# Where independent matmuls stand between an attention's score passes: a set length behind the second scores, and one whole product in every step of the second batch

## The chip, the cores and the metric

One core of one Trainium2 chip runs the program. The metric is device time of one execution in microseconds (us), median of three runs. The profile is one further execution, taken by the hardware profiler. Engines: TensorE (PE; PEld is its weight load), VectorE (DVE), ScalarE (ACT), GpSimd (POOL), SyncE (SP, which only issues DMAs here). PSUM has eight banks of 128 x 512 float32; matmuls write there, VectorE and ScalarE read from there.

## The reference

Input x is 2 batches x 1024 tokens x 1024 channels, all float32.

```python
xn = layernorm(x)                                   # no weights
q, k, v = split(clip(xn @ Wqkv.T, -8, 8))           # each 1024 channels
q, k = layernorm(q) * q_w + q_b, layernorm(k) * k_w + k_b
scores = q_h @ k_h.T * 32**-0.5 + slope_h * (kpos - qpos)   # 32 heads of 32, causal
attn = (softmax(scores) @ v_h) @ Wout.T
ffn = xn @ (mean|W| * sign(W)).T + bias             # W = weight_real, 1024 x 1024
out = x + attn + ffn
```

## The kernel before

Everything is written for one order, laid out by hand: the program issues its instructions in the order in which they shall stand on each engine, and tiles in rotating buffers add the waits.

**The attention** works in blocks (b, qb, g): batch, half of the queries (512) and group of four heads. Four heads of 32 channels stand in the four row strips of TensorE, so that their matmuls run side by side. A block passes twice over its scores. `first_scores` (matmuls at L1006) takes scores of 128 queries against up to 512 keys, four PSUM banks for the four heads, and VectorE finds the row maxima from them (L1025, a custom add-and-max reduction). `shifts` (L1037) turns the maxima into rows of shifts, with small GpSimd operations and a transpose (L1052). `second_scores` makes the scores again, with keys on the partitions (L1067), adds the shifts by tiny matmuls (L1081), masks the diagonal on VectorE (L1100), and ScalarE takes the exponentials into tiles `pT` (L1109, 16 buffers). GpSimd adds those up for the denominators (L1138; VectorE in the very last block). `weigh_values` multiplies `pT` by the values (L1149). `divide` sums over partitions with a matmul `den` (L1168), and ScalarE and GpSimd divide.

**The step loop** (from L1228) takes these units in turn. In step n stand, in this order: the first scores of unit n; `divide` if a block has ended; `weigh_values` of unit n - LAG - 1; the second scores of unit n - LAG, with LAG = 9; and calls of `fill`. Two attention units of different blocks are paired into one where each has less than a bank.

**The fillers.** Everything else on TensorE is a stream of pieces, the generator `pieces`: the projections k, q, v of both batches, then the binarized linear layer, then the output projection. The projections use a seven-product scheme (`seven`, L396): a pair of token tiles needs seven products instead of eight, each of four matmuls of 128 x 128 by 128 x 512 (L402) into one PSUM bank, and VectorE combines them (L433, L444). The linear layer (`mm_f`, L793) has 16 matmuls for one product, in four pieces. `held` is true while a product is half done. `fill(time)` (L903) draws pieces until their estimated costs have used up the time, and every second piece advances the side chains (layer norms, transposes, loads). With `whole` it goes on until the product in hand is done. Overdrawn time is carried over, so a call of `fill` can draw nothing at all.

How much is filled: in the first batch's steps (n < middle = 81), `free` is what an equal share leaves beside the step's own attention work. `BEFORE` = 0.4 of it goes between first and second scores, the rest behind the second scores. In later steps a fixed time `each` goes behind the second scores, nothing between. At the end `fill(inf)` draws all that is left; the last two pairs of the output projection (14 products) need the last block, so they stand there anyway.

**PSUM.** Seven banks (`ps_s`) are shared by first scores (four at a time), second scores (four), the product in hand, transposes and denominators; one bank holds the attention's output. A bank comes free when VectorE or ScalarE has read it.

**Other queues.** SP issues loads in the program's order: q, k and v groups (L930, L934, L943), weights into a ring (L213), and attention outputs back from DRAM for the output projection (L844).

Of the kernel before, what the change touches and what calls it, by code (L numbers as in the profile page):

```python
# [25 lines left out]
def parallel_block_kernel(  # L26
# [49 lines left out]


    ONE, SHORT, TURN = 0.915, 1.03, 0.55
    BEFORE = 0.4
    PART, FOLD, SWITCH = 0.95 / 512, 0.3 / 512, 0.1  # L80
    QK_SCALE = HEAD_DIM ** (-0.5)
    slopes = [2.0 ** (-(h + 1) * ALIBI_BIAS_MAX / N_HEADS) for h in range(N_HEADS)]
# [253 lines left out]
    def advance_sides():  # L336
        time = 0.0
        for s in list(sides):
            cost = next(s, None)
            if cost is None:  # L340
                sides.remove(s)
            else:
                time += cost
        return time
# [49 lines left out]
    held = [False]  # L394
# [498 lines left out]
    def pieces():  # L893
        for b in range(B):
            yield from keys_or_queries("k", b)
            yield from keys_or_queries("q", b)
            yield from values(b)
        yield from binary_linear()
        yield from output()

    left = {"pieces": pieces(), "time": 0.0, "owed": 0.0}

    def fill(time, whole=False, sides_too=True):  # L903

        left["time"] += time
        while left["time"] > 0.0 or (whole and held[0]):
            cost = next(left["pieces"], None)
            if cost is None:  # L910
                left["time"] = 0.0
                break
            left["owed"] += 0.5
            left["time"] -= cost
            if sides_too and left["owed"] >= 1.0:
                left["owed"] -= 1.0
                left["time"] -= advance_sides()

    def fill_until(what):
        while what not in done:  # L920
            left["time"] = 0.0
            fill(0.01)
# [5 lines left out]
    def load_keys(b, qb, g):  # L928
        q = group.tile([P, HALF], FP, tag="q", name=f"qg_{b}_{qb}_{g}", bufs=6)
        nc.sync.dma_start(q, qd[b][g][:, half(qb)])  # L930
        k = []
        for n in range(qb + 1):
            k.append(group.tile([P, HALF], FP, tag="k", name=f"kg_{b}_{qb}_{g}_{n}", bufs=6))
            nc.sync.dma_start(k[n], kd[b][g][:, half(n)])  # L934
        st["q", b, qb, g], st["k", b, qb, g] = q, k

    def load_values(b, qb, g):
        v = []
        for n in range(qb + 1):
            v.append(  # L940
                group.tile([P, NQ, P], FP, tag="v", name=f"vg_{b}_{qb}_{g}_{n}", bufs=4)
            )
            nc.sync.dma_start(  # L943
                v[n],
                vd[b][half(n), g * P : (g + 1) * P].rearrange("(t p) d -> p t d", p=P),
            )
        st["v", b, qb, g] = v

    def open_block(*block):
        st[("mx",) + block] = small.tile(  # L950
            [P, G, NQ], FP, tag="mx", name="mx_{}_{}_{}".format(*block), bufs=3
        )
# [44 lines left out]
    def first_scores(unit):  # L997

        name = "s1_{}_{}_{}_{}_{}".format(*unit[0][0], *unit[0][1:3])
        banks = [score_bank(f"{name}_{j}") for j in range(G)]  # L1000
        c0 = 0
        for block, i, k0, n in unit:
            q, k = st[("q",) + block], st[("k",) + block][k0 // HALF]
            for j in range(G):
                r = slice(32 * j, 32 * j + 32)
                nc.tensor.matmul(  # L1006
                    banks[j][:, c0 : c0 + n],
                    q[r, tokens(i - block[1] * NQ)],
                    k[r, :n],
                    start=True,  # L1010
                    stop=True,
                )
            c0 += n
        for j in range(G):
            c0 = 0
            for block, i, k0, n in unit:
                at = i - block[1] * NQ
                o0 = S - (i + 1) * P + k0
                m = st[("mx",) + block][:, j, at : at + 1]
                sums = work.tile(  # L1020
                    [P, HALF], FP, tag="sums", name=f"sums{name}_{j}_{c0}", bufs=1
                )
                opened = ("max", block, j, i) in st
                st["max", block, j, i] = True
                nc.vector.tensor_tensor_reduce(  # L1025
                    out=sums[:, :n],
                    in0=banks[j][:, c0 : c0 + n],
                    in1=rel[:, o0 : o0 + n],
                    scale=1.0,
                    scalar=m if opened else LOWEST,  # L1030
                    op0=ALU.add,
                    op1=ALU.max,
                    accum_out=m,
                )
                c0 += n

    def shifts(b, qb, g):  # L1037

        mx = st.pop(("mx", b, qb, g))
        sh = small.tile([P, G, NQ], FP, tag="sh", name=f"sh_{b}_{qb}_{g}", bufs=2)  # L1040
        nc.gpsimd.tensor_tensor(sh, mx, pos, ALU.add)
        nc.gpsimd.tensor_scalar(sh, sh, -1.0, None, ALU.mult)
        sb = shift_b.rearrange("p i (j r) -> p j i r", j=G)
        for n in range(3):
            nc.gpsimd.tensor_copy(sb[:, :, :, n], sh)
            if n < 2:
                nc.gpsimd.tensor_tensor(sh, sh, sb[:, :, :, n], ALU.subtract)
        yield True

        ps = ps_s.tile([P, NQ, P], BF, tag="s", name=f"trs_{b}_{qb}_{g}")  # L1050
        for i in range(NQ):
            nc.tensor.transpose(ps[:, i, :], shift_b[:, i, :], ident_b)  # L1052
        rows = small.tile([P, HALF], BF, tag="rows", name=f"rows_{b}_{qb}_{g}", bufs=4)
        nc.scalar.copy(rows, ps.rearrange("p i q -> p (i q)"))
        st["rows", b, qb, g] = rows
# [107 lines left out]
    def divide(b, qb, g):  # L1163

        ps = score_bank(f"den_{b}_{g}_{qb}")
        total = st.pop(("sum", b, qb, g))
        for j in range(G):
            nc.tensor.matmul(  # L1168
                ps[32 * j : 32 * j + 32, :],
                ones,  # L1170
                total[j],
                start=True,
                stop=True,
            )
        inv = work.tile([P, HALF], FP, tag="inv", name=f"inv_{b}_{g}_{qb}", bufs=1)
        nc.scalar.activation(inv, ps, AF.Ln)
        nc.scalar.activation(inv, inv, AF.Exp, scale=-1.0)  # L1177
        ot = st["ot", b, qb, g]
        if (b, qb, g) == blocks[-1]:
            nc.vector.tensor_tensor(ot, ot, inv, ALU.mult)  # L1180
        else:
            nc.gpsimd.tensor_tensor(ot, ot, inv, ALU.mult)  # L1182
            nc.gpsimd.dma_start(od[b][g][:, half(qb)], ot)
        done.add(("o", b, qb, g))
# [32 lines left out]
    def short_lead(block):  # L1217

        return block[1] == 1 and block[2] == 0
# [3 lines left out]
    for n in range(3):  # L1223
        if n in opens:
            load_keys(*opens[n])
    fill(proj - AHEAD * ONE)
    chains = []
    for n in range(steps + 1):  # L1228
        if n + 3 in opens and not short_lead(opens[n + 3]):
            fill_until(("q", opens[n + 3][0]))  # L1230
            load_keys(*opens[n + 3])
        if n + 2 in weighs:
            block = weighs[n + 2]
            fill_until(("v", block[0]))
            load_values(*block)
        if n in opens:
            open_block(*opens[n])
        if n < len(first):
            first_scores(first[n])
        closing = shifts(*closes[n]) if n in closes else None  # L1240
        if closing:
            next(closing)
        m = n - LAG
        if m - 2 in ends:
            divide(*ends[m - 2])
        free = max(share - time_of(n), 0.0)
        if n < middle:
            fill(free * BEFORE, sides_too=False)
        if 0 <= m - 1 < len(second):
            weigh_values(second[m - 1], ends.get(m - 1))  # L1250
        if 0 <= m < len(second):
            second_scores(second[m])
        for c in chains:
            next(c, None)
        chains = [closing] if closing else []
        if n + 2 in opens and short_lead(opens[n + 2]):
            fill_until(("q", opens[n + 2][0]))
            load_keys(*opens[n + 2])
        if n < middle:
            fill(free * (1.0 - BEFORE))  # L1260
        else:
            fill(each, whole=True)
    fill(float("inf"))
# [51 lines left out]
```

## Time and profile before

| | |
|---|---|
| median of 3 runs | 1578.15 us (1576.8 to 1581.82) |
| the profiled execution's own time | 1580.05 us |
| its span, first to last instruction | 1578.3 us |
| mean granted TensorE clock | 0.992 |
| busy: PE, DVE, ACT, POOL | 1553.1, 909.5, 688.5, 998.8 us |

The span begins with the first projection (to about 350 us, with the first first scores from 278 us on), goes on with the first batch's attention over the projections of the second batch (to about 955 us), then the second batch's attention over the linear layer (to about 1235 us) and over the output projection (to about 1520 us), and ends with the last 14 or 15 products. A group of matmuls in the timeline is drawn from its first start to its last end, waits inside it included.

### The profile page before, as it was taken

What the parts mean: (1) busy time and instruction counts of PE and PEld (TensorE: products, weight loads), DVE (VectorE), ACT (ScalarE), POOL (GpSimd) and SP (SyncE); (2) the same over time, 40 slices, a digit from 0 to 9 for tenths busy, and PEclk for the clock granted to TensorE, in tenths of its full rate; (3) what the DMA queues carried; (4) which work ended last, traced back from release to release, by engine and by line L of the source; (5) the groups of instructions that cost most, each with busy time, mean ns of one, the idle gap of its engine ahead of it and who ended that gap; (6) DMA issues with size and microseconds to landing.
All of it is one profiled execution on the core that took longest, in us unless ns stands there. A gap on an engine that the chain in (4) does not pass through costs nothing.

```text
span 1578.3 us, 25307 instructions
## 1 busy us (share of the span) xinstructions
PE 1553.1 (98%) x8452; PEld 682.3 (43%) x8452; DVE 909.5 (58%) x2602; ACT 688.5 (44%) x1425; POOL 998.8 (63%) x1306
## 2 busy tenths in 40 slices
PE   7999999999999999999999999999999999999998
PEld 3444444444444434333333344555555433333343
DVE  7745353766676666666666555656555556555232
ACT  2553341114665645545542374545444434434420
POOL 4473071024675566676566599887798988778841
PEclk9999999999999999999999999999899999999999
DMA  7776364592323655558742377656565831233232
GB/s 290 295 254 261 100 206 151 185 324 74 107 95 112 224 191 182 131 129 253 249 159 94 115 250 221 140 130 136 134 147 97 225 87 39 77 81 74 57 78 53
DMA packets 116466, 244.94 MB, mean 155 GB/s; under 512 B 10544, under 2 KB 50992, under 8 KB 113008
## 3 DMA queue, kind: packets, MB, share of 16 engines
q1 hardware_dynamic: 88752, 145.01, 27.8%
q0 software_dynamic: 27584, 98.32, 24.0%
q8 instruction: 67, 1.10, 0.3%
q14 instruction: 63, 0.52, 0.1%
HBM read 155.47 MB, written 107.74 MB: 167 GB/s over the span
## 4 chain that ended last, share of the span: by engine, by line
PE 65%; DVE 1%; POOL 1%; issue 1%; ACT 1%; DMA 0%; POOLq 0%; DVEq 0%; ACTq 0%
PE s L1006 9%; PE s L1067 9%; PE o L1149 8%; PE mm_f L793 8%; PE mm_o_t L402 7%; PE mm_o L402 5%; PE mm_q_t L402 4%; PE mm_v_t L402 4%; PE mm_q L402 3%; PE mm_v L402 3%; PE den L1168 2%; PE s L1081 2%; PE mm_k_t L402 1%; PE mm_k L402 0%; PE tr_q L506 0%
## 5 line engine op out<-in xcount | busy, mean ns | idle before, releaser
L1138 POOL TENSOR_TENSOR pT<-pT,pT 128x512 f32<-128x512 f32 (+3 forms) x628 | 579.9, 983 | 101.8 <-ACT pT L1109 100.9
L1109 ACT ACTIVATE pT<-s,kpos 128x512 f32<-128x512 f32 (+3 forms) x768 | 378.2, 590 | 464.5 <-DVE s L1100 274.1
L1025 DVE CUSTOM_DVE_ANT_0 sumss<-s,rel 128x512 f32<-128x512 f32 (+2 forms) x284 | 179.1, 631 | 112.4 <-PE s L1006 79.3
L1006 PE MATMUL s<-kg,qg 32*128 32x512 f32 (+3 forms) x1536 | 197.3, 523 | 0.7 <-ACT kT L570 0.6
L1067 PE MATMUL s<-qg,kg 32*128 32x512 f32 (+3 forms) x1536 | 176.7, 525 | 1.3 <-DVE mx L1025 1.3
L1149 PE MATMUL o<-pT,vg 128*32 128x512 f32 (+3 forms) x1536 | 155.3, 499 | 0.0
L793 PE MATMUL mm_f<-sg,hl 128*128 128x512 f32 x512 | 128.6, 403 | 2.1 <-DVE mx L1025 2.1
L1006 PEld LDWEIGHTS s<-kg,qg 32*128 32x128 f32 x1536 | 80.0, 183 | 110.4 <-issue 44.8
L1100 DVE TENSOR_TENSOR s<-s,behind 128x256 f32<-128x256 f32 (+1 forms) x320 | 96.9, 371 | 48.1 <-PE s L1081 47.9
L402 PE MATMUL mm_o_t<-w_o_t,ot 128*128 128x512 f32 x256 | 116.6, 602 | 0.0
L1067 PEld LDWEIGHTS s<-qg,kg 32*128 32x128 f32 x1536 | 71.7, 185 | 101.4 <-issue 56.3
L1182 POOL TENSOR_TENSOR ot<-ot,inv 128x512 f32<-128x512 f32 x31 | 39.5, 1273 | 114.3 <-ACT inv L1177 114.3
L402 PE MATMUL mm_k_t<-w_k_t,xT 128*128 128x512 f32 x224 | 110.7, 614 | 0.5 <-DVE mx L1025 0.4
L793 PEld LDWEIGHTS mm_f<-sg,hl 128*128 128x128 f32 x512 | 94.7, 190 | 34.4 <-DVE mx L1025 10.6
L402 PE MATMUL mm_q_t<-w_q_t,xp 128*128 128x512 f32 x224 | 108.2, 605 | 0.0
L402 PE MATMUL mm_v_t<-w_v_t,xp 128*128 128x512 f32 x224 | 106.3, 606 | 0.1
L402 PE MATMUL mm_k<-w_k,xT 128*128 128x512 f32 x192 | 91.4, 616 | 0.9 <-DVE mx L1025 0.7
L402 PE MATMUL mm_v<-w_v,xp 128*128 128x512 f32 x192 | 89.6, 604 | 0.0
L1149 PEld LDWEIGHTS o<-pT,vg 128*32 128x32 f32 x1536 | 37.3, 109 | 119.1 <-issue 102.8
L402 PE MATMUL mm_q<-w_q,xp 128*128 128x512 f32 x192 | 88.7, 603 | 0.0
L402 PE MATMUL mm_o<-w_o,ot 128*128 128x512 f32 x192 | 87.5, 602 | 0.1
L1025 DVE CUSTOM_DVE_ANT_0 umss<-s,rel 128x512 f32<-128x512 f32 x100 | 69.2, 692 | 26.1 <-PE s L1006 15.3
(222 smaller groups left out, 2009.0 us busy)
## 6 DMA issues: line engine op xcount, KB each, us to landing
xp<-xd SPq DMA_DIRECT2D x16, 1792.0 KB, 8.3
kg<-kd SPq DMA_DIRECT2D x48, 256.0 KB, 5.0
vg<-vd SPq DMA_DIRECT2D x48, 256.0 KB, 7.9
wd_ot<-in_wout_t_dram POOLq DMA_DIRECT2D x11, 1024.0 KB, 9.4
xd<-xT POOLq DMA_DIRECT2D x8, 1280.0 KB, 5.3
x<-in_x_dram SPq DMA_DIRECT2D x16, 512.0 KB, 6.3
kd<-kT POOLq DMA_DIRECT2D x16, 512.0 KB, 4.1
qd<-qT POOLq DMA_DIRECT2D x16, 512.0 KB, 4.2
```

The costliest lines, as they stand in the source:

```text
L402: nc.tensor.matmul(ps, pr[:, FACTOR[block], c, :], W[what, block, c], start=(c == 0), stop=(c == NI - 1),)
L793: nc.tensor.matmul(ps, hl[c // NI][:, m % 2, c % NI, :].bitcast(FR), sg[n, c], start=(m == 0), stop=(m == 2 * NC - 1),)
L1006: nc.tensor.matmul(banks[j][:, c0 : c0 + n], q[r, tokens(i - block[1] * NQ)], k[r, :n], start=True, stop=True,)
L1025: nc.vector.tensor_tensor_reduce(out=sums[:, :n], in0=banks[j][:, c0 : c0 + n], in1=rel[:, o0 : o0 + n], scale=1.0, scalar=m if opened els ...
L1067: nc.tensor.matmul(banks[j][:, c0:c1], k[r, tokens(kt % NQ)], q[r, q0:], start=(c0 == 0), stop=False,)
L1081: nc.tensor.matmul(banks[j][:, c0:c1], ones_b[r, :], rows[r, q0:], start=False, stop=(c1 == HALF or (block, kt, q0) == unit[-1]),)
L1100: nc.vector.tensor_tensor(at, at, mask, ALU.add)
L1109: nc.scalar.activation(pT[:, c0:c1], banks[j][:, c0:c1], AF.Exp, bias=kpos[:, h, a : a + 1], scale=slopes[h],)
L1138: eng.tensor_tensor(part_sum, part_sum, pT[j], ALU.add)
L1149: nc.tensor.matmul(po[32 * j : 32 * j + 32, q0:], v[:, kt % NQ, 32 * j : 32 * j + 32], pT[j], start=(kt == 0), stop=(last is not None and ...
L1168: nc.tensor.matmul(ps[32 * j : 32 * j + 32, :], ones, total[j], start=True, stop=True,)
L1182: nc.gpsimd.tensor_tensor(ot, ot, inv, ALU.mult)
```

## The change

Three edits, all in how the stream of pieces is dealt out. In the first batch, the fill behind the second scores gets a set length `LATER` = 4.0 (in the estimate's us, or all of `free` where that is less), and the rest goes between first and second scores. In the second batch, a call with `whole` draws at least one piece, and so at least one whole product, whatever time was overdrawn before. No instruction is added or removed; they stand in another order.

```diff
-    BEFORE = 0.4
+    LATER = 4.0
...
         left["time"] += time
-        while left["time"] > 0.0 or (whole and held[0]):
+        none = whole
+        while left["time"] > 0.0 or none or (whole and held[0]):
+            none = False
             cost = next(left["pieces"], None)
...
         free = max(share - time_of(n), 0.0)
         if n < middle:
-            fill(free * BEFORE, sides_too=False)
+            fill(max(free - LATER, 0.0), sides_too=False)
...
         if n < middle:
-            fill(free * (1.0 - BEFORE))
+            fill(min(free, LATER))
         else:
             fill(each, whole=True)
```

## The prediction

> **What bounds the kernel now.** I read the page first, then the granted clock by stretches, then TensorE's timeline step by step, and last the end of the run. TensorE counts as busy nearly all the time:
>
> ```profile
> PE 1553.1 (98%) x8452; PEld 682.3 (43%) x8452; DVE 909.5 (58%) x2602; ACT 688.5 (44%) x1425; POOL 998.8 (63%) x1306
> ```
>
> All of its work is the same before and after, so only its stalls can change. They hide inside "busy": a group of matmuls that waits for PSUM banks is drawn as one long group. In the second batch a normal step costs 7.2 to 8.5 us and holds one product (3.85 us of `mm_f`). Three steps hold none, those that end near 1052, 1125 and 1203 us. Here is the first of them, in the timeline (start, length, engine, line, tile, form, count):
>
> ```profile
> 1049.18 1.15 PE L1006 MATMUL s<-kg,qg 32*128 32x256 f32 x16
> ...
> 1050.83 1.27 PE L1067 MATMUL s<-qg,kg 32*128 32x512 f32 x7
> ...
> 1052.45 4.73 PE L1006 MATMUL s<-kg,qg 32*128 32x512 f32 x8
> ...
> 1057.11 1.93 PE L1168 MATMUL den<-pT,ones 128*32 128x512 f32 x8
> ...
> 1058.82 2.79 PE L1149 MATMUL o<-pT,vg 128*32 128x512 f32 x16
> ...
> 1061.54 1.70 PE L1067 MATMUL s<-qg,kg 32*128 32x384 f32 x16
> ```
>
> Second scores are followed at once by the next first scores. These want banks that VectorE (the maxima, L1025) and ScalarE (the exponentials, L1109) still read, so eight matmuls that take 1.07 us elsewhere take 4.66. After that even groups without a wait are twice as long: `den` 1.71 instead of 0.88, `o` 2.72 instead of 1.40. The stretches (length, then PE, PEld, DVE, ACT, POOL busy with counts, then granted clock) say why:
>
> ```profile
> 1049.00:1067.00 18.00, 18.00 (x110) 7.85 (x108) 9.08 (x33) 9.34 (x21) 13.61 (x22) 0.81 0.56 105
> 1067.00:1122.00 55.00, 54.58 (x442) 32.34 (x444) 34.45 (x108) 28.14 (x61) 42.95 (x59) 1.00 0.68 154
> 1122.00:1140.00 18.00, 18.00 (x104) 8.85 (x104) 9.42 (x34) 7.87 (x18) 11.65 (x21) 0.72 0.40 86
> ```
>
> Thin matmul work behind the empty step makes the granted clock fall, and it stays down: 18 x (1 - 0.81) / 0.5 is about 7 us at half speed, 18 x 0.28 / 0.5 about 10. The third empty step kept clock 1.00.
>
> **The change, part by part.** *(1) A product in every step of the second batch.* In the changed instruction order all three empty steps carry a product. I price each from neighbours of the same shape. Around 1052: the two steps now take 3.27 + 14.78 = 18.05 us with one product; the same two shapes at 1008 and 1015 take 7.35 + 8.51 = 15.86 with two. The added product is 3.85 that leaves another place, so the gain is 18.05 + 3.85 - 15.86 = 6.0. Around 1125: 3.39 + 14.51 = 17.90; with a product each their groups, at their lengths elsewhere, come to 7.27 + 7.21, gain 17.90 + 3.85 - 14.48 = 7.3. Around 1203: 2.82 + 0.47 + 9.64 = 12.93 against 6.80 + 8.49, gain 1.5. Sum **-14.8**. Beside it VectorE and ScalarE are half idle (34 and 28 of 55 us), so nothing of theirs is late next; GpSimd is a rival below.
>
> *(2) The first batch: products moved from between the two scores to behind the second ones.* By the instruction order most steps from 350 to 955 us go from two pieces (one piece is a matmul of 0.86) between and three behind to one and four; 15 steps of 69 get none between. A step now:
>
> ```profile
> 753.05 1.14 PE L1006 MATMUL s<-kg,qg 32*128 32x512 f32 x8
> 754.12 1.98 PE L402 MATMUL mm_q_t<-w_q_t,xp 128*128 128x512 f32 x4
> 756.03 1.06 PE L1149 MATMUL o<-pT,vg 128*32 128x512 f32 x8
> 757.03 1.15 PE L1067 MATMUL s<-qg,kg 32*128 32x384 f32 x16
> ...
> 758.57 2.79 PE L402 MATMUL mm_q<-w_q,xp 128*128 128x512 f32 x6
> ...
> 760.05 3.03 ACT L1109 ACTIVATE pT<-s,kpos 128x384 f32<-128x384 f32 x8 [6.79 <-DVE s L1100]
> ...
> 761.29 2.23 PE L1006 MATMUL s<-kg,qg 32*128 32x512 f32 x8
> ```
>
> The last line waits for the exponentials: 2.18 to the next group instead of 1.07. Such excess of L1006 over 1.07 sums to 23.4 us up to 985, most of it before 560 (1.31, 1.82, 1.38, 0.97, ...). Each is shortened by at most what the fill ahead of it grows, nearly always 0.86 and at times 1.3 to 1.7; the sum of the smaller of the two over the 23 late steps is **-17.7**.
>
> The other side: second scores (L1067) come 0.86 us earlier after their first scores in 48 steps, 1.7 to 1.9 earlier in 17 (0.86 per matmul, and 0.19 for the entry into a product). They need banks that L1025 releases. For each step I took the start of each L1067 matmul less the end of the VectorE or ScalarE instruction it depends on. In the 48 steps this slack has a mean of 1.32 us (0.05 to 2.68), in the 17 a mean of 1.53. Where the shift exceeds it, PE waits the rest: ten steps, 4.6 us, and thirteen, 7.9 us: **+12.5**. Queued behind that wait on PE are only that step's second scores and its products; VectorE's masks and ScalarE's exponentials wait with them. The three steps of the turn from projections to `mm_f` (955 to 985) lose all or half of what lies between: the same arithmetic says 4.6, but steps after 985 of the same shape have nothing between and do not wait at all, so between 0 and 4.6 I take **+2**. A product that is entered once a step instead of twice saves 0.19 (1.91 for two matmuls against 1.72 inside a product): entries fall from 190 to 176, **-2.7**. Sum of part 2: -17.7 + 12.5 + 2 - 2.7 = **-5.9**; with slacks 0.5 smaller +9.3, with 0.5 larger -13.7.
>
> *(3) The end.* Three products are used up earlier, so the last attention steps have none: two lay between the last second scores and `den`, one behind it. Now:
>
> ```profile
> 1510.63 3.70 PE L402 MATMUL mm_o_t<-w_o_t,ot 128*128 128x512 f32 x8
> ...
> 1511.32 3.03 ACT L1109 ACTIVATE pT<-s,kpos 128x384 f32<-128x384 f32 x8 [3.64 <-DVE s L1100]
> ...
> 1514.19 1.37 DVE L1138 TENSOR_TENSOR pT<-pT,pT 128x384 f32<-128x384 f32 x5 [0.17 <-ACT pT L1109]
> ...
> 1515.27 3.70 PE L402 MATMUL mm_o_t<-w_o_t,ot 128*128 128x512 f32 x8
> ...
> 1518.90 1.06 PE L1168 MATMUL den<-pT,ones 128*32 128x512 f32 x8
> ```
>
> Without them the chain scores, exponentials (to 1514.35), last additions (to 1515.56), `den` stands bare: 4.95 us from 1510.63, of which the `o` matmuls fill 1.0. That is **+4.0**. Behind `den`, the division and VectorE's small copies end some 5 us later, under two products (7 us) that do not need them: nothing. The thin 5 us resemble the 3.5 us from 1052 that brought the clock down; the shortest drop at 1049 to 1140 is 7 us at half speed, costing 3.4 if PE is full, and the 2.2 us stall at 1203 cost nothing. Between 0 and 3.4 I take **+1.7**.
>
> [...]
>
> *(4) Queues.* On SP the loads of `ot` for the output pairs stand ahead of some key and value loads that stood ahead of them. Four such loads took 3.14 us at 1337, and those tiles are wanted two to three steps (14 us and more) later: nothing. Side chains advance by pieces, whose number is the same.
>
> **The sum.** -14.8 - 5.9 + 5.7 = -15.0 from the profiled execution's 1580.05 (span 1578.3): 1565.05. That execution lies 1.9 above the median of the runs, 1578.15, so I predict **1563**.
>
> **Rivals.** *GpSimd takes over (0.14).* From 985 to 1240 it is busy 214 of 255 us. With the stalls gone that is 214 of 240, 89%, and it owns the additions L1138 that free the exponentials' buffers. For it: 98% busy from 1213 to 1240 (26.55 of 27). Against: in that stretch PE does not stall, and ScalarE's idle time before L1109 is put down to VectorE. If it gives back half of part 1: 1563 + 7.4 = 1570.
>
> *Second scores wait for the maxima all through the first batch (0.12), slower.* The place is L1067 behind L1025, the price what part 2's slacks leave. If VectorE is later than now, because products end at other points of the step and their two or three evictions of 0.69 us get ahead of the maxima, slacks shrink: by 0.5 us the waits sum to 27.7 instead of 12.5, by 0.75 to 38.6. It decides from 0.5 us on, where the whole gain of 15 is gone; at 0.75 the time is 1563 + 26 = 1589. For it: seven steps have a slack under 0.3 already. Against: the mean is 1.3, and the same fill moved behind the masks also frees VectorE ahead of them.
>
> That the change does not do what it says is excluded for the empty steps by the instruction order; for the first batch the set length of 4.0 leaves one piece between, often none.
>
> **The numbers.** Forecast 0.74, rivals 0.14 and 0.12. What this measurement tells from no change is about 0.3%, 4.7 us. The forecast is faster save for 0.02; the GpSimd rival lies near the bound, 0.08 faster and 0.05 within; the slower rival gives 0.03 within, the rest beyond. Together faster 0.80, within 0.10, slower 0.10. The range: part 2's two ends are 15 up and 8 down, part 3's are 2 either way, GpSimd 7 up; leaving out 2 in 10 I take 1553 to 1577.
>
> **What would show it.** Right: granted clock 1.00 from 985 to 1500; no L1006 group over 2 us there; L1006's excess before 985 near 6 us, with about 12 us of new excess at L1067; `den` of the last block some 5 us behind the last scores. Wrong: L1067 excess of 28 us or more; GpSimd above 95% with L1006 waiting for L1109 in the second batch; or new clock drops in the first batch.

## The result and the profile after

The changed kernel takes 1588.34 us in the median of 5 runs (1586.48 to 1593.54), the kernel before 1578.9 us in the 5 runs beside them: ratio 1.006, 95% interval 1.0042 to 1.0077. It is slower by 9.4 us where 15 us of gain were forecast, outside the range. In this kernel's numbering two is added to every line after L907 (first scores L1008, maxima L1027, second scores L1069, shift rows L1083, shift transposes L1054, `den` L1170). The page of its profiled execution (span 1584.6, 6.3 more than before) shows the same busy share as before:

```profile
PE 1554.1 (98%) x8452; PEld 686.5 (43%) x8452; DVE 912.1 (58%) x2602; ACT 688.6 (43%) x1425; POOL 997.9 (63%) x1306
```

So again only stalls inside "busy" can differ. The formerly empty steps first, in the stretches (length, then PE, PEld, DVE, ACT, POOL busy with counts, then granted clock), and the first of them in the timeline:

```profile
1061.00:1077.00 16.00, 16.00 (x129) 9.40 (x131) 9.89 (x35) 9.56 (x21) 11.96 (x20) 1.00 0.80 143
1130.00:1146.00 16.00, 16.00 (x127) 10.63 (x129) 10.72 (x38) 9.75 (x23) 13.81 (x22) 1.00 0.61 130
```

```profile
1061.03 1.15 PE L1008 MATMUL s<-kg,qg 32*128 32x256 f32 x16
...
1064.52 3.92 PE L793 MATMUL mm_f<-sg,hl 128*128 128x512 f32 x16
1068.37 1.14 PE L1008 MATMUL s<-kg,qg 32*128 32x512 f32 x8
1069.44 1.06 PE L1170 MATMUL den<-pT,ones 128*32 128x512 f32 x8
```

The first scores that took 4.73 take 1.14, `den` 1.06, and the clock is 1.00. What came back elsewhere shows in a table that I made by adding up the steps (start of a step to start of the next), with the excess of each kind: first scores over 1.07 a step, second scores and shift rows over 1.29.

| us, profiled execution | before | after |
|---|---|---|
| steps 9 to 29 (350 to 555): time; excess first, second scores | 202.4; 15.8, 6.5 | 205.3; 5.2, 17.5 |
| steps 30 to 76 (to 947 or 954): time; excess first, second | 394.4; 5.1, 0.6 | 398.0; 1.1, 10.6 |
| the turn, steps 77 to 81: time; excess first, second | 45.0; 2.5, 1.8 | 49.2; 0.7, 6.3 |
| three formerly empty steps, net of their products | 0 | -14.6 |
| the step at the shift transposes near 1249 | | +4.5 |
| the end, net of three products | 0 | +4.5 |

With 0.6 before step 9 and 0.5 behind the turn the differences (2.9, 3.6, 4.2, -14.6, 4.5, 4.5) make 6.2 of the 6.3. The two profiled executions lie 3 us closer together than the medians. Of the turn's second scores and shift rows, 2.0 us after and 1.0 before are a wait of shift transposes for GpSimd. The clock is part of the loss: before, three stretches at half clock (3.41, 6.83 and 10.24 us) up to the end of the attention; after, seven (3.41, but 6.83 at 522), four of them before 555 us, two in the turn, one at 1249. The median granted clock of the runs is 0.988, against 0.993 in 86 runs of the kernel before: span times the missing share is 19 us against 11. Among runs of one kernel each such us makes a run 0.7 us longer (the slope over all runs here), so by this estimate about 6 of the 9.4 us are seen through the clock.

### The profile page after: what moved, and what is told of

The parts are those of the page before. It is cut to its first block, busy times and chain, and to the rows that moved or that the text cites. A ratio compares the mean times of both kernels' runs of the same rounds, so it can differ in the third digit from the quotient of the medians.

```text
span 1584.6 us, 25321 instructions
## 1 busy us (share of the span) xinstructions
PE 1554.1 (98%) x8452; PEld 686.5 (43%) x8452; DVE 912.1 (58%) x2602; ACT 688.6 (43%) x1425; POOL 997.9 (63%) x1306
## 4 chain that ended last, share of the span: by engine, by line
PE 66%; DVE 1%; POOL 1%; issue 1%; ACT 1%; POOLq 0%; DVEq 0%; ACTq 0%
PE s L1069 9%; PE s L1008 8%; PE mm_f L793 8%; PE o L1151 8%; PE mm_o_t L402 7%; PE mm_o L402 5%; PE mm_q_t L402 4%; PE mm_v_t L402 4%; PE mm_q L402 3%; PE mm_v L402 3%; PE s L1083 2%; PE den L1170 2%; PE mm_k_t L402 2%; PE mm_k L402 1%; PE tr_q L506 0%
## 5 line engine op out<-in xcount | busy, mean ns | idle before, releaser
L1027 DVE CUSTOM_DVE_ANT_0 sumss<-s,rel 128x512 f32<-128x512 f32 (+2 forms) x284 | 178.9, 630 | 107.2 <-PE s L1008 76.5
L1069 PE MATMUL s<-qg,kg 32*128 32x512 f32 (+3 forms) x1536 | 198.8, 524 | 2.2 <-DVE mx L1027 1.7
L1008 PE MATMUL s<-kg,qg 32*128 32x512 f32 (+3 forms) x1536 | 173.1, 521 | 0.2
L1069 PEld LDWEIGHTS s<-qg,kg 32*128 32x128 f32 x1536 | 81.2, 184 | 114.3 <-issue 51.6
L1008 PEld LDWEIGHTS s<-kg,qg 32*128 32x128 f32 x1536 | 69.6, 184 | 105.5 <-issue 57.7
L1027 DVE CUSTOM_DVE_ANT_0 umss<-s,rel 128x512 f32<-128x512 f32 x100 | 69.1, 691 | 27.0 <-PE s L1008 16.2
```

Of the source, the lines that this page charges most:

```text
L1008: nc.tensor.matmul(banks[j][:, c0 : c0 + n], q[r, tokens(i - block[1] * NQ)], k[r, :n], start=True, stop=True,)
L1027: nc.vector.tensor_tensor_reduce(out=sums[:, :n], in0=banks[j][:, c0 : c0 + n], in1=rel[:, o0 : o0 + n], scale=1.0, scalar=m if opened els ...
L1069: nc.tensor.matmul(banks[j][:, c0:c1], k[r, tokens(kt % NQ)], q[r, q0:], start=(c0 == 0), stop=False,)
```

## The experiments

Times are medians; the ratio to the kernel before on the same chip has its 95% interval in brackets.

**The two parts alone.** The kernel before with only this edit:

```diff
-        while left["time"] > 0.0 or (whole and held[0]):
+        none = whole
+        while left["time"] > 0.0 or none or (whole and held[0]):
+            none = False
```

> The second-batch edit alone; the first batch keeps the 0.4 split. Theory A (the first batch's new split costs some 11 us through second scores that wait for maxima; the second-batch edit gains as forecast): the three stretches gain 14.5, the bare tail costs 4.5, the wait of a shift transpose near 1249 us costs 4.5, so about 5.5 us less than before: a median near 1573, and 15 us below the changed kernel. Theory B (the product in every step is what costs, through GpSimd and clock drops that are spread over the run): 1585 or more.

Measured 1578.68 against 1580.61, ratio 0.9988 [0.9975, 1.0001]. And the changed kernel without it, with `LATER` alone:

> The first-batch edit alone; the second batch's steps may again have no product. Theory A: some 11 us more than before, 1589 to 1590, all of it before 985 us, with the waits in second scores as in the changed kernel. Theory B: 1579 or less, as forecast blind (a gain of 6 us: 1573).

Measured 1588.39, ratio 1.0043 [1.003, 1.0056]. The second part loses, as theory A has it: its first batch shows the changed kernel's excesses again (17.3 and 10.6 at second scores). The first part gains almost nothing (1.9 us, not clear of noise), which theory A did not have. Its trace, of an execution 3.5 us above its median, has the three steps as forecast, but 6.0 us more at the shift transposes, 4.5 at the end, and 3.5 in the turn, where the instructions stand in the order of before but half clock falls at 959 and 976 us.

**What second scores wait for.** In steps before the turn the maxima run over half the keys (the other half is left out, and the exponentials are scaled flat so that they stay finite), in the changed kernel and in the kernel before:

```diff
+                nm = n // 2 if now[0] < middle else n
...
-                    out=sums[:, :n],
+                    out=sums[:, :nm],
```

> The changed kernel, with the maxima of the first batch's steps taken over half of each row only, and scores that weigh nothing in the exponentials (this leaves out part of the softmax; instruction counts and the other sizes stay). A 512-wide maximum takes 0.7 us, a half one about 0.43. Theory A (second scores wait for banks that the maxima still read): the excess of second scores over 1.29 us per step, 17.5 + 10.6 us from 350 to 955 us, falls below 8. Theory C (they wait for ScalarE, or for VectorE's evictions of the projections): it stays above 20.

> The kernel before with the same half maxima: the control for the run on the changed kernel. Its second scores' excess is 7.1 us from 350 to 955 us, nearly all in four early steps, and its first scores' 20.9. Theory A: second scores' excess below 3; the first scores' excess, which waits for exponentials, falls by less than half. With both kernels freed of the maxima, theory A says that the changed one is the shorter one up to 955 us, by 5 us or more; theory C that it still is the longer one.

Measured, one run each: 1558.21 and 1562.06. VectorE's time in maxima up to 985 us falls from 247 to 169 us. The excess at second scores in steps 9 to 76 of the changed kernel falls from 28.1 to 14.8 (more than theory A's 8, less than theory C's 20); steps 9 to 76 take 581.4 with the new split and 586.3 with the old. So neither theory's figure came: maxima a third shorter take away about half of the wait, and what the rest waits for these runs do not tell. With faster maxima the new split is the better one by 5 us, in one run each.

**The steps with nothing between.** Fifteen steps of the changed kernel get no piece between the scores. Here each gets at least one:

```diff
-            fill(max(free - LATER, 0.0), sides_too=False)
+            here = max(free - LATER, 0.05 - left["time"])
+            fill(here, sides_too=False)
...
-            fill(min(free, LATER))
+            fill(free - here)
```

> The changed kernel, but every step of the first batch gets at least one piece between first and second scores (15 steps have none in the changed kernel). Theory A (a step with nothing between leaves the second scores too little slack, and a late bank then costs the lone matmul and its lone follower besides): in the changed kernel the eleven such steps after 555 us have 8.2 us of excess at second scores and shift rows, 0.74 each, and the 36 with one piece 2.4, 0.07 each; here the eleven cost under 1.5 together, and the stretch 555 to 947 comes down by 6 to 7 us, the four before 555 by 1 to 2; time about 1580, no different from the kernel before. Rival B (what counts is the larger fill behind second scores, which makes VectorE's evictions pile up there): excess falls by less than 3, time 1586 or more.

Measured 1580.91, ratio 1.0006 [0.9996, 1.0016]: theory A. Steps 30 to 76 fall from 398.0 to 393.2 us (excess at second scores 10.6 to 3.6), which is below the kernel before. One such step, from the timeline of the changed kernel and then of this one:

```profile
641.12 1.14 PE L1008 MATMUL s<-kg,qg 32*128 32x512 f32 x8
642.19 1.06 PE L1151 MATMUL o<-pT,vg 128*32 128x512 f32 x8
...
643.12 0.69 DVE L1027 CUSTOM_DVE_ANT_0 sumss<-s,rel 128x512 f32<-128x512 f32 x1
643.18 1.38 PE L1069 MATMUL s<-qg,kg 32*128 32x512 f32 x7
...
644.14 0.39 PE L1083 MATMUL s<-rows,ones_b 3*128 3x512 bf16 x3
644.40 0.59 PE L1069 MATMUL s<-qg,kg 32*128 32x512 f32 x1
...
644.83 0.38 PE L1083 MATMUL s<-rows,ones_b 3*128 3x512 bf16 x1
```

```profile
638.15 1.14 PE L1008 MATMUL s<-kg,qg 32*128 32x512 f32 x8
639.22 1.12 PE L402 MATMUL mm_q_t<-w_q_t,xp 128*128 128x512 f32 x2
...
640.28 1.07 PE L1151 MATMUL o<-pT,vg 128*32 128x512 f32 x8
...
641.27 1.14 PE L1069 MATMUL s<-qg,kg 32*128 32x512 f32 x8
...
642.24 0.40 PE L1083 MATMUL s<-rows,ones_b 3*128 3x512 bf16 x4
```

A count of 8 is four matmuls, each in two records, here called its two passes, and the four strips go side by side: in the single records of the second fence all four first passes start together at 641.27, and the maxima that free their banks are out by then. In the first fence three strips start at 643.18, and the fourth at 643.87, when the second maximum (643.12 + 0.69) has left its bank. Its second pass then runs alone from 644.40, its shift row alone from 644.83, and scores and rows take 1.96 us from start to start in place of 1.29: the strip was 0.69 late, and 0.67 is lost.

**The stall near 1249 us.** In the changed kernel, from the timeline:

```profile
1246.39 1.26 POOL L392 TENSOR_TENSOR ot<-ot 128x512 f32<-128x512 f32 x1
1247.61 0.22 POOL L1043 TENSOR_TENSOR sh<-mx,pos 128x16 f32<-128x16 f32 x1
...
1249.50 0.25 POOL L1047 CAST shift_b<-sh 128x16 bf16<-128x16 f32 x1
...
1249.81 0.61 PE L1054 MATMUL trs<-ident_b,shift_b 128*128 128x128 bf16 x4 [3.25 <-POOL shift_b L1047]
```

GpSimd's four sums of an output pair (L388 to L392) now stand ahead of the shift rows that PE wants; in the kernel before they stood behind:

```profile
1234.25 0.26 POOL L1045 CAST shift_b<-sh 128x16 bf16<-128x16 f32 x1
1234.40 4.97 POOL L1138 TENSOR_TENSOR pT<-pT,pT 128x512 f32<-128x512 f32 x4
1239.32 1.29 POOL L388 TENSOR_TENSOR ot<-ot 128x512 f32<-128x512 f32 x1
```

The first trial puts all pair sums off by four side steps in the changed kernel:

```diff
-            yield 0.0
-            yield 0.0
+            for _ in range(6):
+                yield 0.0
             add_up(pr, nc.gpsimd, 0, parts)
```

> The changed kernel with GpSimd's four sums of the output pair put off, so that they stand behind the shift rows of the next block and not ahead of them. Theory A (the stall near 1249 us in the changed kernel, 3.25 us at the shift transposes and about 1.3 more of half clock behind it, is GpSimd's order of work alone): stall gone, about 4.5 us shorter than the changed kernel, 1584 where the kernel before takes 1580. Rival B (GpSimd's load is too high now that the empty steps are filled, so that whatever stands ahead of the shifts is late): the stall stays within 1 us of 3.25, at this or a neighbouring place, time 1588.

Measured 1589.88, ratio 1.0058 [1.0035, 1.0081]: the stall is gone in the trace (that step takes 7.41, not 11.91), and the time has not moved. The same edit beside the product alone, and beside the one piece between:

> The kernel before with the product in every step of the second batch and the pair sums put off behind the shift rows; nothing else. Theory A (the product alone gained 14.5 in the three steps and gave back 4.5 to 6.5 at the shift transposes): 1578.7 - 4.5 to 6.5 = 1572 to 1574, unless the bare end at 1520 to 1528, where the changed kernel with late sums lost 6 us to half clock, takes it (then 1578). Rival B (the run with late sums was not faster because the stall was hidden by something else): 1578 to 1580 with a full clock at the end.

> The changed kernel with one piece at least between the scores and the pair sums put off. Theory A: 1580.9 - 4.5 = about 1576, up to 1580 where the bare end loses its clock. The bare end itself takes 3.6 us for the o matmuls and 1.55 for den at full clock, 7.1 and 4.0 at half.

Measured 1580.39 (1.0007 [0.9997, 1.0017]) and 1580.69 (1.0004 [0.9993, 1.0015]): no gain either. The end took it. From the timelines, the end of the changed kernel, then of the last of these runs:

```profile
1524.43 3.24 PE L1151 MATMUL o<-pT,vg 128*32 128x384 f32 x16 [1.25 <-ACT pT L1111]
1524.61 3.90 DVE L1140 TENSOR_TENSOR pT<-pT,pT 128x384 f32<-128x384 f32 x8
...
1528.04 1.62 PE L1170 MATMUL den<-pT,ones 128*32 128x512 f32 x8 [0.37 <-DVE pT L1140]
```

```profile
1513.62 8.94 DVE L1140 TENSOR_TENSOR pT<-pT,pT 128x384 f32<-128x384 f32 x8
...
1519.02 1.20 POOL L389 TENSOR_TENSOR ot<-ot 128x384 f32<-128x384 f32 x1
1520.18 1.04 POOL L391 TENSOR_TENSOR ot<-ot 128x384 f32<-128x384 f32 x1
...
1520.51 4.08 PE L1170 MATMUL den<-pT,ones 128*32 128x512 f32 x8 [3.82 <-DVE pT L1140]
```

The last pairs' sums, put off too, now run beside VectorE's last additions, which take 8.94 us in place of 3.90, and `den` waits 3.82. From the last `o` matmuls' start to the product behind `den` this run takes 11.1 us in place of 5.2. My expectation had called that loss half clock, and was wrong on its cause: half clock falls there too, but from 1521.70 us on, behind the wait. So the same edit for all pairs but the last block's (`range(2 if (b, qb) == blocks[-1][:2] else 6)`), in the changed kernel:

> The changed kernel, with the pair sums put off except those of the last block, which stay where they were. Theory A (the stall at the shift transposes costs its 4.5 us, and the run with all sums put off lost 6 at the end because GpSimd's last sums ran beside VectorE's last additions): the end takes 3.6 (o) and 1.55 (den) as in the changed kernel, and the time is about 1588.3 - 4.5 = 1584. Rival B (half clock comes back at the end whenever the stall at 1249 is gone): o and den at the end take 7.1 and 4.0, time 1588.

Measured 1583.4, ratio 1.0014 [1.0001, 1.0026]: theory A. That is 4.9 us under the changed kernel by the medians, 7 by the ratios, so the stall was worth its 4.5 us or somewhat more.

**The end.** One product more for it, first by a budget of 12 pieces fewer in the first batch (`- 12 * ONE` on `fills`), on the product alone and on the one piece between, with all sums late:

> The kernel before with the product in every step of the second batch, GpSimd's pair sums put off behind the shift rows, and 12 pieces fewer in the first batch's budget, which leaves one product more for the last attention step. Theory A: the gain of part 1 was 14.5 and was given back by the stall at the shift transposes (4.5 to 6.5) and at the end (4.5); both gone, the time is 1580.6 - 14.5 + 1 = about 1567, at most 1572 if clock drops in the first batch and the turn take some of it. Rival B (the kernel gives gains in the second batch back wherever next its clock falls): 1576 or more, like the product alone.

> The changed kernel with one piece at least between the scores, the pair sums put off and 12 pieces fewer in the first batch. Theory A: 1588 - 4.5 (stall) - 3.5 (end) - 8 (steps without a piece between) = about 1572; against the kernel before with the product, the late sums and the kept end it is decided by whether one piece between is dearer (second scores) or cheaper (first scores) than two: by the excesses after 555 us it would be 1.4 us cheaper there, and about as dear before 555. Rival B: over 1578.

Measured 1579.74 (0.9998 [0.9989, 1.0008]) and 1581.97 (1.002 [1.0005, 1.0035]): misses, though the end is covered. Pieces missing in the first batch cost more than the product missing at the end. Up to the end of the turn (steps 9 to 81) about one product less is done than in the two runs with late sums, and yet it takes 651.0 us for 643.3 and 653.7 for 646.2: steps 30 to 76 take 398.3 in both, the turn 54.5 and 56.4. Then by leaving one late step, of the shape whose empty form cost 1.5 in the kernel before, without its product, and last with the turn split as before:

```diff
-        else:
+        elif n != len(first) - 10:
             fill(each, whole=True)
```

```diff
+            if n >= middle - 4:
+                here = 0.4 * free
```

> As the run with one piece between and late sums, but one step of the shape whose empty form cost 1.5 us in the kernel before (the one near 1203) goes without its product near 1395 us, so that one product more is left for between the last second scores and den. Theory A: the empty step costs 1.5, the end gains 2.5 at full clock and 6 to 8 where it had lost its clock: 1575 or less, and fewer half-clock windows behind 1500 us. Rival B (any empty step loses its clock): 1580.

> As the run with the covered end, but the last four steps of the first batch are split as in the kernel before (0.4 between). In the changed kernel these steps and the next two take 49.2 us, in the kernel before 45.0. Theory A (the turn's loss is the second scores left without cover: 6.3 us of excess against 1.8): the turn comes back to 45 to 46, 2 to 3 us under the run with the covered end: 1572 to 1573. Rival B (the turn's loss is half clock that falls there in any order, as it did in the kernel with the product alone, 48.5 us with the same order as before): no change.

Measured 1574.15 (0.996 [0.9945, 0.9975]) and 1572.97 (0.9958 [0.9943, 0.9974]). Covering the end with that product is worth 6.5 us with the sums as they stand there. The turn falls from 47.3 to 45.6 us in the traces, but the two intervals overlap: unclear as a time.

**Old split or new.** With the sums, the end and the product mended, all of the first batch as before; and the old split only before step 30 and in the turn, one piece between in the steps from 30 on:

> The kernel before with the product in every step of the second batch but one (near 1390), whose product goes to the end, and the pair sums put off except the last block's: the first batch as in the kernel before. Theory A (the second batch is where all of the gain is; the new split with one piece at least is worth no more than 1 us against the old): 1572 to 1574, like the run with one piece between. Rival B (the new split with one piece is better by the first scores' 13 us): 1580 or more.

> As the run with the turn as before, but the steps before the 30th are split as in the kernel before too, and the last block's sums stay. By the tables of excess: before 555 us 202.4 to 203.5 against 205.8 (no half clock at 375 to 400, 455 and 521), from 555 to 947 us 393.2 against the 394.4 of the old split. Theory A: 1570 to 1571, 2 us under the run with the turn as before and 1 to 2 under the old split. Rival B: within 1 us of the old split all the same, since the clock drops elsewhere.

Measured 1572.29 (0.9949 [0.9932, 0.9966]) and 1566.42 (0.9919 [0.9903, 0.9935]). The mixed kernel is the fastest of those that take the whole maxima, 13.6 us under the kernel before, and 5.9 under the old split, more than either theory had. Only the order of steps 30 to 76 differs between these two, and in their traces those steps are 1.3 us apart (394.3 and 393.0). The turn, in the same order in both, is 3.6 apart (48.0 and 44.4): half clock falls there at 960 and 977 us with the old split and not in the mixed kernel. Why it does so is not shown, so of the 5.9 us only the 1.3 is traced to the split. Stretches of the mixed kernel's trace:

```profile
350.00:555.00 205.00, 202.05 (x1274) 86.70 (x1266) 138.51 (x441) 116.97 (x258) 117.60 (x187) 0.98 0.38 127
555.00:947.00 392.00, 392.00 (x2264) 147.75 (x2260) 248.42 (x712) 198.81 (x407) 263.76 (x311) 1.00 0.58 175
985.00:1240.00 255.00, 252.91 (x1928) 143.33 (x1924) 154.05 (x491) 125.05 (x259) 221.59 (x293) 1.00 0.66 153
1240.00:1500.00 260.00, 259.96 (x1562) 98.61 (x1555) 134.32 (x390) 111.86 (x212) 213.12 (x238) 1.00 0.28 66
```

The granted clock is 0.98 in the first of them and 1.00 in the other three. For the early steps the traces lean to the old split without settling it: steps 9 to 29 take 202.4 to 204.2 us in the five comparable traces that have it there, and 202.7 to 205.8 in the four with one piece at least. One step is dearer with the new split in all of them (12.9 to 14.6 us for 9.5). At 516 us the changed kernel (first fence) has one matmul between the scores (a count of two), the mixed kernel (second) three (a count of six), as before:

```profile
517.36 1.13 PE L402 MATMUL mm_k<-w_k,xT 128*128 128x512 f32 x2
...
521.11 0.69 PE L1069 MATMUL s<-qg,kg 32*128 32x256 f32 x2 [0.64 <-DVE mx L1027]
522.22 1.64 PE L1069 MATMUL s<-qg,kg 32*128 32x256 f32 x9 [0.41 <-DVE mx L1027]
...
524.64 5.02 PE L402 MATMUL mm_k<-w_k,xT 128*128 128x512 f32 x6
```

```profile
516.74 2.84 PE L402 MATMUL mm_k<-w_k,xT 128*128 128x512 f32 x6
...
521.56 0.91 PE L1069 MATMUL s<-qg,kg 32*128 32x256 f32 x9 [0.34 <-DVE mx L1027]
```

There second scores wait 3.8 us in place of 1.6 from first to last, the clock falls to half at 522.24 for 6.83 us, and three matmuls (six records of 0.43 us at full clock) behind the wait take 4.86 from start to start: the step takes 14.61 us, in the mixed kernel 9.53.

## Why the prediction was wrong

**Part 1 was right.** The three steps gave 6.0, 7.3 and 1.25: 14.6 for 14.8, and their clock stayed full (1.00 in each).

**Part 2: the gain was right, the price not.** First scores' excess before 985 us is 7.1 ("near 6"), 16.3 gained for 17.7. New excess at second scores is 25.5 where 12.5 and 2 were put down, 21.0 of it in the 68 steps that the 12.5 was summed over, so that term was sized at little more than half. The step that failed is "I took the start of each L1067 matmul less the end of the VectorE or ScalarE instruction it depends on". I gave the eight records of a group to the four matmuls in pairs, so the third and fourth matmul seemed to start 0.53 later than the first. But the first four records are the first passes of the four strips, and all four matmuls start together. The slack of the third and fourth, which need the later maxima, was 0.53 too large. Read rightly, the same trace of before has a mean slack of 0.90 in place of 1.40, and the same sum gives 28.5. It then hits some steps (one at 638 us before: 0.62 worked out, 0.67 measured; at 687: 0.71 and 0.76; at 737: 1.25 and 1.30; at 788: 1.26 and 1.31), where the old sum had 0.09, 0.18, 0.72 and 0.73. It is too high elsewhere. Where first scores were late before, they now start earlier and their maxima with them. At 621 us before, where they were not late, 0.80 is worked out and none was measured: VectorE's other work ahead of the maxima moved as well, and the first maximum, which started 2.10 us after the first scores, now starts 1.23 after them. So 28.5 was too much by a third.

So the second rival was the case, though not as it argued: slacks were 0.5 smaller not by a later VectorE but from the start, and its price for 0.5, 27.7, stood in the text. The half-maxima runs show that shorter maxima on VectorE take about half of that wait away.

**A term was missing: clock.** New half clock in the first batch was listed as what would make the forecast wrong, but the sum has none for it. It came four times before 555 us (3.41, 3.41, 3.41 and 6.83 us), and twice in the turn (3.41 each). I had priced half clock behind thin work only at the end, where it did not come: behind 1249 us the changed kernel has none before 1580.37. That thin work sets it off was my estimate from the two stretches with a clock of 0.81 and 0.72; no run shows it apart from the waits beside it. At 516 us the loss is 5.1 us, of which 2.9 lie in second scores and shift rows and the rest in the slow matmuls behind them.

**Part 3 was near, part 4 wrong.** The end lost 4.5 for 4.0 + 1.7: the bare chain cost that, and the 1.7 for the clock did not come. `den` starts 5.1 us behind the end of the last scores. "Side chains advance by pieces, whose number is the same" made the queues free: but with products three places earlier the pair sums came ahead of the shifts on GpSimd, and 4.5 us of stall was priced at nothing. It is order in one queue and not GpSimd's load, which is 85% from 985 to 1240 (215.9 of 255), so the rival that GpSimd takes over did not come either.

What stays open: why the product alone, which takes away the 17 us of half clock in the empty steps, has a median clock of only 0.9945 in its 12 runs against 0.993. Its trace shows half clock at 959 and 976 us in unchanged work; which executions get it there was not settled.

## What to carry to other kernels

A filler that is moved buys slack at one wait and sells it at another. Read the slack that is sold from single records, with passes and strips told apart, and from the member of the group that starts with the others but depends on the last release; then add the clock that may be lost behind it (in the step at 516 us half clock for 6.83 us), and look at what each side queue now has ahead of the operation that the critical engine wants next. One piece in every gap was worth more here than a set length that leaves some gaps empty (1580.91 us against 1588.34).

## What the runs showed of the hardware

In the profiled executions of the two kernels half clock came for 3.41, 6.83 or 10.24 us at a time, save the last time in each, which reaches past the last instruction (from 1574.70 us on in the kernel before, from 1580.37 in the changed one). Up to there every change of the granted clock lies a whole multiple of 3.4133 us, to within 0.002, from the first one (at 359.56 and 358.40 us). Half clock came both with and without idle time of PE. At 1055.88 and 1127.56 us in the kernel before PE counts as busy in all 18.00 us of the stretch around it; at 1249.28 us in the changed kernel it had been idle for 2.7 us, since the last shift row ended at 1246.56. What sets it off is not shown.

VectorE's last additions take 0.54 (128 x 384) and 0.28 us (128 x 128) by themselves in the changed kernel; in the run whose `den` waits 3.82 they take 1.35 to 1.91 and 1.07 beside GpSimd's sums, and seven of the eight end 0.41 to 0.43 (128 x 384) or about 0.15 us (128 x 128) after one of GpSimd's. In the changed kernel the first of them, the only one beside a GpSimd addition (1524.36 to 1525.86), takes 1.68 and ends 0.43 after it. Why they end so is not shown.
